# Graph attention on one core: values of two key blocks issued together ahead of the scores of every second step

## Chip, cores, metric

One core of one Trainium2 chip. The metric is device time in microseconds (us), median over runs. Runs of one kernel differ by up to some 0.2%. The traces show the array's clock halved for a few intervals of 3.4 us that fall differently in every run; over the runs of the kernel before, the mean granted clock lies between 0.996 and 0.999, and the shorter spans have the higher clock.

Engine names: PE is TensorE's matmuls, PEld its weight loads, DVE VectorE, ACT ScalarE, POOL GpSimd, SP SyncE (it issues most DMAs). L481 is line 481 of the kernel.

## The reference, cut

32 batches of 512 nodes with 512 features. Layer 0 is a graph convolution, layer 1 attention with 8 heads that sees only neighbours; each is added to its input and normalised.

```python
x = layernorm(x + deg * (x @ Wi.T + b) + adj @ (x @ Wj.T))
q, k, v = heads(x @ Wq.T + bq), heads(x @ Wk.T + bk), heads(x @ Wv.T + bv)   # 8 heads of 64
s = where(adj == 0, -inf, q @ k.T / 8)
x = layernorm(x + merge(softmax(s) @ v) @ Wo.T + bo)
```

## The kernel before

The attention of batch b runs in 8 steps, one for each half g of the heads (4 heads) and each block kc of 128 keys. Between the attention matmuls of a step the kernel places "pieces": products of the projections of neighbouring batches, spread over the steps so that PE always has work. Two PSUM buffers (mma, mmb) take the pieces in turn.

```python
    def scores(b, hp, kc):                        # two heads
        ps = sc_tile()                            # PSUM, two buffers
        for s in range(2):
            r = slice(s * HD, (s + 1) * HD)       # 64 rows of the array each
            nc.tensor.matmul(ps[:, s, :], KT[b, hp // 2][r, ...], QT[b, hp // 2][r, ...], ...)
        e = E[hp % 2, kc] = work([P, 2, N], "e", 4)
        nc.scalar.activation(ps, ps, AF.Exp, scale=QSCALE)              # L485
        nc.vector.tensor_tensor(e, ps, edge[...], op=OP.mult)           # L486: mask

    def values(b, g, kc):                         # four heads, 32 columns of the array each
        if kc == 0:
            PV[g] = [ov_tile(), ov_tile()]        # PSUM, two buffers in all
        for r in range(2):
            for h in range(4):
                nc.tensor.matmul(PV[g][r][32 * h:32 * h + 32, :], V[b][:, kc, c0:c0 + 32], E[h // 2, kc][...], ...)

    for n in range(1, B + 1):                     # cut: flushes, the last batch's exceptions
        b = n - 1
        for step in range(STEPS):
            g, kc = divmod(step, NC)
            scores(b, 2 * g, kc)
            scores(b, 2 * g + 1, kc)
            # pb, pg, pk: the step before
            values(pb, pg, pk)
            if pk == NC - 1:
                sums(pg)                          # L513: sums of exponentials, into a buffer of sc
                drain(pb, pg)                     # L518: ACT takes them out
                extra = rest(pb, pg)              # 4 reciprocals, 2 scalings into oT (L538), a check
            for f in PERIODS[n][step]: ...        # pieces, and small jobs of the other engines
```

## Time and profile before

| | before |
|---|---|
| median of 4 runs | 3709.5 us (3708.7 to 3709.9) |
| PE busy; share of the chain that ended last | 99%; 96% |
| DVE, POOL, ACT busy | 65%, 53%, 28% |
| values blocks between scores and pieces | 255 |

A line of the timeline gives start, length, engine, line, operation, output<-input, shape, count and, in brackets, the engine's idle time before it with what ended it. A float32 matmul leaves two records, so 8 matmuls of values show as x16. The lengths overlap from one record to the next: PE's pace is read from starts. The prediction below shows the page and the timelines.

### The profile page before, as it was taken

Reading aid. Unit: us, or ns where it says so; the run is one execution under the profiler, and the core shown is the slowest. Engines: PE = TensorE matmul, PEld = TensorE weight load, DVE = VectorE, ACT = ScalarE, POOL = GpSimd, SP = SyncE. Lnnn points to the kernel's source line nnn. Section 1 sums busy time; section 2 is a strip of 40 time slices with the busy share of each in tenths; the row PEclk is TensorE's granted clock in tenths of the full one; section 3 lists DMA queues with packets and bytes.
Section 4 is the critical chain, followed back from the end, with each engine's and each line's share of the span. In section 5 each row is a group of like instructions: output and inputs, shape, how many; then the busy total and the mean of one; then the engine's idle time right before and its main releaser. Section 6 shows DMA issues by size and latency. Waiting matters only on the chain.

```text
span 3706.9 us, 49623 instructions
## 1 busy us (share of the span) xinstructions
PE 3665.2 (99%) x18458; PEld 2511.4 (68%) x18458; DVE 2396.9 (65%) x3139; ACT 1029.1 (28%) x1482; POOL 1946.5 (53%) x1986
## 2 busy tenths in 40 slices
PE   8999999999999999999999999999999999999997
PEld 5666666666676767676666767676767666666763
DVE  4566766666666666666666666666666666666666
ACT  2222232222322222323233222222232332222322
POOL 3465545555455564455554555644555545556443
PEclk9999999999999999999999999999999999999999
DMA  7444556455555545554555544455545555445541
GB/s 250 125 126 133 151 151 162 124 141 138 152 159 145 128 135 150 153 160 120 141 142 154 159 141 130 134 151 157 157 122 139 141 159 157 137 132 137 151 131 44
DMA packets 797174, 530.02 MB, mean 143 GB/s; under 512 B 530433, under 2 KB 611841, under 8 KB 796929
## 3 DMA queue, kind: packets, MB, share of 16 engines
q1 hardware_dynamic: 780384, 494.78, 49.4%
q10 hardware_dynamic: 16320, 31.46, 2.3%
q8 instruction: 151, 2.47, 0.3%
q14 instruction: 95, 0.77, 0.1%
q0 software_dynamic: 224, 0.53, 0.0%
HBM read 453.25 MB, written 73.40 MB: 142 GB/s over the span
## 4 chain that ended last, share of the span: by engine, by line
PE 96%; DVE 1%; SPq 1%; POOL 1%; DMA 0%; issue 0%; ACT 0%; POOLq 0%; DVEq 0%; ACTq 0%
PE mma L427 31%; PE mmb L427 31%; PE sc L481 13%; PE ov L503 13%; PE mmb L325 3%; PE mma L325 3%; PE sc L513 2%; SPq L113 0%; DMA wv<-e 0%; DVE e L486 0%; DVE rl L522 0%; DVE st L289 0%; SPq L144 0%; PE sc L721 0%; SPq L166 0%
## 5 line engine op out<-in xcount | busy, mean ns | idle before, releaser
L485 ACT ACTIVATE sc<-sc 128x1024 f32<-128x1024 f32 x512 | 493.1, 1006 | 1538.4 <-PE sc L481 1532.2
L486 DVE TENSOR_TENSOR e<-sc,edge 128x1024 f32<-128x1024 f32 x512 | 602.5, 1218 | 211.4 <-ACT sc L485 180.4
L427 PE MATMUL mmb<-ring,big 128*128 128x256 f32 x3144 | 733.7, 382 | 3.1 <-issue 3.1
L427 PE MATMUL mma<-ring,big 128*128 128x256 f32 x3112 | 724.5, 381 | 3.9 <-ACT p L434 2.8
L427 PEld LDWEIGHTS mmb<-ring,big 128*128 128x128 f32 x3144 | 593.7, 190 | 134.1 <-issue 30.2
L427 PEld LDWEIGHTS mma<-ring,big 128*128 128x128 f32 x3112 | 585.7, 190 | 135.6 <-issue 27.0
L481 PE MATMUL sc<-q,k 64*128 64x512 f32 x2048 | 509.7, 616 | 0.0
L396 POOL TENSOR_TENSOR big<-big 128x512 f32<-128x512 f32 x376 | 493.1, 1339 | 29.3 <-ACT big L354 10.1
L503 PE MATMUL ov<-e,v 128*32 128x512 f32 x4096 | 494.0, 600 | 3.6 <-DVE oT L538 3.6
L492 POOL TENSOR_TENSOR es<-e 128x1024 f32<-128x1024 f32 x128 | 301.0, 2364 | 346.0 <-DVE e L486 346.0
L427 PE MATMUL mma<-big,ring 128*128 128x256 f32 x1808 | 431.5, 382 | 3.2 <-DVE k L465 3.2
L427 PE MATMUL mmb<-big,ring 128*128 128x256 f32 x1776 | 422.7, 381 | 0.0
L291 POOL TENSOR_SCALAR mv<-mv 128x1 f32<-128x1 f32 x256 | 51.0, 199 | 672.5 <-DVE mv L290 660.0
L427 PEld LDWEIGHTS mma<-big,ring 128*128 128x128 f32 x1808 | 341.0, 190 | 76.8 <-issue 25.1
L427 PEld LDWEIGHTS mmb<-big,ring 128*128 128x128 f32 x1776 | 334.5, 190 | 72.0 <-issue 25.1
L503 PEld LDWEIGHTS ov<-e,v 128*32 128x32 f32 x4096 | 107.1, 109 | 351.6 <-issue 321.7
L204 POOL TENSOR_TENSOR xlo<-xh,xhi 128x512 fp32r<-128x512 f32 x128 | 164.0, 1294 | 337.3 <-ACT xhi L203 337.2
L481 PEld LDWEIGHTS sc<-q,k 64*128 64x128 f32 x2048 | 176.5, 186 | 208.4 <-issue 205.4
L340 POOL TENSOR_TENSOR big<-big,deg_r 128x512 f32<-128x512 f32 x124 | 174.0, 1404 | 266.5 <-DVE big L339 266.5
L494 DVE TENSOR_TENSOR es<-es,e 128x1024 f32<-128x1024 f32 x251 | 307.7, 1227 | 0.0
L445 DVE TENSOR_TENSOR xh<-xh,mma 128x512 f32<-128x512 f32 x186 | 126.7, 681 | 269.7 <-PE mma L427 269.7
L445 DVE TENSOR_TENSOR xh<-xh,mmb 128x512 f32<-128x512 f32 x186 | 126.7, 681 | 262.6 <-PE mmb L427 262.6
(147 smaller groups left out, 3659.5 us busy)
## 6 DMA issues: line engine op xcount, KB each, us to landing
ring<-wo SPq DMA_DIRECT2D x217, 256.0 KB, 2.8
ring<-wq SPq DMA_DIRECT2D x160, 256.0 KB, 3.9
ring<-wv SPq DMA_DIRECT2D x160, 256.0 KB, 3.3
ring<-wk SPq DMA_DIRECT2D x160, 256.0 KB, 3.4
ring<-wi SPq DMA_DIRECT2D x155, 256.0 KB, 2.7
ring<-wj SPq DMA_DIRECT2D x155, 256.0 KB, 2.6
xh<-in_x_dram SPq DMA_DIRECT2D x32, 1024.0 KB, 5.5
xa<-in_x_dram SPq DMA_DIRECT2D x124, 256.0 KB, 3.9
```

What stands on the lines that cost most here:

```text
L204: nc.gpsimd.tensor_sub(lo, xs, hi.bitcast(FT))
L325: nc.tensor.matmul(pm, parts[w][:, jc, :], adjR[:, jc, :], start=(w == 0 and jc == 0), stop=(w == 1 and jc == NC - 1))
L340: nc.gpsimd.tensor_tensor(XD[b][:, dc, :], XD[b][:, dc, :], deg_r, op=OP.mult)
L396: nc.gpsimd.tensor_tensor(dst, p, q, op=OP.subtract)
L427: nc.tensor.matmul(pm[:, c * Q:(c + 1) * Q], lhs, rhs, start=first, stop=(kc == 1 and n == len(terms) - 1), skip_group_check=True)
L445: nc.vector.tensor_tensor(d, d, pm, op=OP.add)
L481: nc.tensor.matmul(ps[:, s, :], KT[b, hp // 2][r, hp % 2, kc * P:(kc + 1) * P], QT[b, hp // 2][r, hp % 2, :], start=True, stop=True)
L485: nc.scalar.activation(ps, ps, AF.Exp, scale=QSCALE)
L486: nc.vector.tensor_tensor(e, ps, edge[:, kc:kc + 1, :].to_broadcast([P, 2, N]), op=OP.mult)
L492: nc.gpsimd.tensor_add(ES[i], E[i, 0], E[i, 1])
L494: (eng or nc.vector).tensor_add(ES[i], ES[i], E[i, kc])
L503: nc.tensor.matmul(PV[g][r][32 * h:32 * h + 32, :], V[b][:, kc, c0:c0 + 32], E[h // 2, kc][:, h % 2, :], start=(kc == 0), stop=(kc == NC - 1))
```

## The change

The intent: every change between the array's cuts (64\*128 for scores, 128\*32 for values, 128\*128 for pieces) costs PE time. If the values of two steps stand together, every second step is spared one visit to the values' cut. Even steps issue the two waiting blocks, then their scores; odd steps issue scores alone. The last batch keeps the old order.

```diff
+    due = []
     for n in range(1, B + 1):
         ...
-            scores(b, 2 * g, kc)
-            scores(b, 2 * g + 1, kc)
-            pb, pg, pk = (b, *divmod(step - 1, NC)) if step > 0 else (b - 1, 1, NC - 1)
-            if pb >= 0:
-                values(pb, pg, pk)
-                ... sums, drain, rest after the last block
+            alone = b == B - 1 and step > 0
+            if alone:
+                scores(b, 2 * g, kc)
+                scores(b, 2 * g + 1, kc)
+            if alone or kc % 2 == 0:
+                for pb, pg, pk in due:
+                    values(pb, pg, pk)
+                    ... sums, drain, rest after the last block
+                due = []
+            due.append((b, g, kc))
+            if not alone:
+                scores(b, 2 * g, kc)
+                scores(b, 2 * g + 1, kc)
```

More of the change, by code (lines that the diff above doesn't have):

```diff
@@ L758, in gnn_attention_kernel @@
             g, kc = divmod(step, NC)
-            scores(b, 2 * g, kc)
-            scores(b, 2 * g + 1, kc)
-            pb, pg, pk = (b, *divmod(step - 1, NC)) if step > 0 else (b - 1, 1, NC - 1)
-            if pb >= 0:
-                values(pb, pg, pk)
-                if pk == NC - 1:
-                    sums(pg)
-                    drain(pb, pg)
-                    extra = rest(pb, pg)
+            alone = b == B - 1 and step > 0
[5 more added lines that the diff above has]
+                    values(pb, pg, pk)
+                    if pk == NC - 1:
+                        sums(pg)
+                        drain(pb, pg)
+                        extra = rest(pb, pg)
+                due = []
[3 more added lines that the diff above has]
+                scores(b, 2 * g + 1, kc)
             late = [(presum, i, kc) for i in range(2) if kc > 0]
```

## The prediction

> **What bounds the kernel now.** I read the page first: engine shares, then the chain that ended last.
>
> ```profile
> PE 3665.2 (99%) x18458; PEld 2511.4 (68%) x18458; DVE 2396.9 (65%) x3139; ACT 1029.1 (28%) x1482; POOL 1946.5 (53%) x1986
> PE 96%; DVE 1%; SPq 1%; POOL 1%; DMA 0%; issue 0%; ACT 0%; POOLq 0%; DVEq 0%; ACTq 0%
> ```
>
> PE is the bound from end to end: 99% busy and 96% of the chain. Only the time between PE's starts counts; other engines matter when they hold PE up. Next I looked at one step (there are 256, eight to each of 32 batches) in the timeline of PE alone. A step has a scores block (L481), a values block (L503), then "pieces", the products of the projections (L427, L325).
>
> ```profile
> 1823.14 1.99 PE L481 MATMUL sc<-q,k 64*128 64x512 f32 x8
> 1825.06 1.92 PE L503 MATMUL ov<-e,v 128*32 128x512 f32 x16
> 1826.91 0.48 PE L427 MATMUL mma<-ring,big 128*128 128x256 f32 x1
> ```
>
> The shapes 64\*128, 128\*32 and 128\*128 are three ways of cutting up the array. The timeline of weight loads gives the rhythm inside a block:
>
> ```profile
> 1823.68 0.19 PEld L481 LDWEIGHTS sc<-q,k 64*128 64x128 f32 x2 [0.24 <-issue]
> 1824.11 0.19 PEld L481 LDWEIGHTS sc<-q,k 64*128 64x128 f32 x2 [0.23 <-issue]
> 1825.06 0.16 PEld L503 LDWEIGHTS ov<-e,v 128*32 128x32 f32 x8 [0.76 <-issue]
> 1825.51 0.13 PEld L503 LDWEIGHTS ov<-e,v 128*32 128x32 f32 x4 [0.30 <-issue]
> ```
>
> Each block is four rounds 0.43 us apart, but its first round is longer: 0.54 us for scores (1823.14 to 1823.68), 0.45 us for values (1825.06 to 1825.51). And each block is longer than its rounds: scores 1.92 us from start to next block's start, values 1.85 us, against 4 x 0.43 = 1.72. A step whose values are followed by the sums of exponentials (L513, the same cut) shows what is absent when the cut stays:
>
> ```profile
> 1809.82 1.92 PE L503 MATMUL ov<-e,v 128*32 128x512 f32 x16
> 1811.56 1.04 PE L513 MATMUL sc<-es,ones 128*32 128x512 f32 x8
> ```
>
> Here values take 1.74 us, not 1.85: 0.11 us is the price of leaving the cut, and the remaining 0.02 to 0.03 is the longer first round. So a change of cut costs a drain (0.09 to 0.11 us) plus a first weight load that nothing hides (0.10 us for 128 columns, 0.026 us for 32). Over all steps I measured from PE's starts, piece to scores 0.197, scores to values 0.121, values to piece 0.217: nearly the same in all 250 cases. PE has almost no other lost time after the first 140 us.
>
> **What the Trainium skill says.** "TensorEngine Tiling (Array Packing)", Key Properties: changing the tiling mode drains the TensorE, using another tile of the same mode does not. The trace agrees: 1.85 against 1.74 us above. "TensorE: Matmul & The Clock Gate", LDWEIGHTS: a load costs its columns over 1.2 per ns, which is 107 ns for 128 columns and 27 for 32. The lengthened first rounds (about 0.105 and 0.026 us) agree, although a load's own record is longer (0.19). The same page, Part 1, has VectorE and ScalarE as strict FIFOs. The trace agrees: the vector engine's work below runs back to back in program order while PE needs the last item of it.
>
> **The change, part by part.** Today 255 values blocks stand each between scores and pieces. Afterwards the values of two steps stand together before the scores of every even step; odd steps have none. The last batch keeps the old order from its second step on. No matmul goes; 31 x 4 = 124 separate values blocks go, merged into a neighbour. A merged block pays no entry load and no exit drain: 0.026 + 0.11 = 0.138 us. The same sum by transitions (piece to values estimated at 0.091 + 0.026 = 0.117, values to scores at 0.217, scores to piece 0.200 as the very first step shows) is 136.6 us of switches before, 119.4 after. **Gain: 124 x 0.138 = 17.1 us.**
>
> Against it stands what moves. In odd steps nothing now lies between scores and pieces, so the pieces start 1.85 us sooner after the scores (1.92 us instead of 3.77). In even steps too the pieces follow the scores directly. The exponentials (ACT, L485) and the masking (DVE, L486) depend on the scores, so in both they end about 2.7 to 2.9 us after pieces begin, not 0.8 to 1.1. I therefore took every wait of PE on another engine and asked whether its slack beats 1.85 us; a bank's next load starts about 0.054 us after its reader ends, and a held first load adds its 0.105. In even steps I found enough room. Three places in odd steps do not:
>
> Step 7, timeline of DVE:
>
> ```profile
> 1797.39 2.35 DVE L486 TENSOR_TENSOR e<-sc,edge 128x1024 f32<-128x1024 f32 x2
> 1799.66 0.70 DVE L339 STREAM_TRANSPOSE big<-xa 128x512 f32<-128x512 f32 x1
> 1800.29 2.40 DVE L345 SCALAR_TENSOR_TENSOR xh<-b_r,deg_c,xh 128x512 f32<-128x512 f32 x2
> 1802.61 1.21 DVE L494 TENSOR_TENSOR es<-es,e 128x1024 f32<-128x1024 f32 x1
> 1803.74 0.68 DVE L465 TENSOR_TENSOR k<-mmb,k 128x512 f32<-128x512 f32 x1
> ```
>
> The queue has no gap, so bank mmb comes free at 1804.42, counted from scores that start at 1795.17. PE's next use of it is at 1806.08 today: 1.66 us of slack. Less 1.85 that is -0.19; with 0.054 and 0.105, PE stalls 0.35 us. Some 30 batches: 10.4 us.
>
> Step 3: the first piece (today at 1855.57) reads the turned activations that the transpose of L373 finishes at 1853.86 (1852.61 + 1.25). It would like to start at 1853.72: a stall of 0.14 + 0.054 = 0.19 us, 30 times: 5.8 us (its first load is exposed in any case).
>
> Step 5: masking ends at 1884.44; the add L465 behind it (0.69) would free mmb near 1885.05, while PE wants it at 1885.07 instead of 1886.92. With the load, a stall of about 0.15 us, 30 times: 4.5 us.
>
> One new wait: in steps 0 and 4 sums now come before the scores and take one of the two sc buffers, so the second scores tile waits until ACT has drained the sums (L518, 0.60 us and 0.09 more for its accumulator). From the recorded offsets the drain ends 0.14 us before PE wants the buffer; the held load makes it about 0.02 us, 62 times: 1.5 us.
>
> Sum: -17.1 + 10.4 + 5.8 + 4.5 + 1.5 = **+5 us**, that is 3714 us if every stall comes as worked out.
>
> **Rivals.** (a) Switches only: the stalls don't show, because DVE's items can run faster when they fall at other moments beside GpSimd (the pair of L345 takes 2.40 us here and 3.42 a step earlier, both with POOL busy). Then 3709 - 17 = 3692 us. For it: the switch costs are very regular and their number is exact. Against it: the three chains are recorded item by item, and an early step shows PE idle for 0.78 us on just such a DVE add (138.2 us). (b) The lag is larger than I think: a further wait that I take as covered binds, for instance L470 in step 4, whose bank would come free within 0.1 us of PE's need, or the drain holds both scores tiles (62 x 0.4 = 25 us). Then 3720 to 3740 us. (c) Waits of values on the scaled outputs vanish (L538 released weight loads in about 35 cases). I count nothing: these are idle times of the load path, while PE's own starts show no delay there.
>
> **Range and chances.** The two main terms are of the same size, 17 us for and 22 us against; I know the first better (within 5 us), the second within about 10. Weighing (a) at a third brings the centre to 3709 us. The range runs from (a) to the weak form of (b): 3692 to 3721. 2% is 74 us, which no path reaches except by a wait that I have missed altogether.
>
> **What would show it.** Right: the PE timeline shows 32 values records in one block of about 3.57 us, scores going straight over to pieces in 1.92 us, fewer separate blocks (131); in odd steps idle of PE or its weight load put down to DVE L465 (steps 5 and 7) and L373 (step 3), with sums near 15, and 5 us. Wrong: values blocks no shorter per step than today (then the piece-to-values switch costs more than 0.12 us); no PE idle behind L465 and L373 (rival a); or large waits on ACT L518, L470 or POOL (rival b).

## More of the kernel before

Lines of the periods that matter later (z marks a job that is no piece):

```python
 # phase_a, steps 6 and 7: gathers (L325) g, pieces k, transposes, bias additions (base, L345)
            res += g[i:i + 1] + k[i:i + 1] + [z(l0_turn, n, i)]
            if i in (1, 2):
                res += [z(base, n, i - 1)]
 # phase_b, end of step 1 and step 2 (DVE comes to h_turn in step 3): layer 0 is normalised (apply, L296, ACT), stored to HBM (L360), read
 # back in another layout (L367) and transposed by DVE (h_turn, L373), for the projections
        ... *project(m, 7), z(apply, n, 0), z(h_store, n, 0), l0[5], z(h_load, n, 0), z(add_bo, n - 1, 1), *project(m, 4),
            l0[3], z(stats, n, 1), z(h_turn, n, 0), *project(m, 5)]
 # phase_c, from step 3: v[1] is the first piece that reads the transpose
```

## The result, and the profile after

| | before | after |
|---|---|---|
| median of 4 runs | 3709.5 us | 3755.2 us (3753.8 to 3758.1) |
| ratio to before | 1 | 1.0126 (95% interval 1.0111 to 1.0141) |

A ratio is the mean time of one kernel's fast runs over that of the other's fast runs of the same rounds, so not quite the ratio of these medians. The kernel became 46 us slower: within 2%, but clear of noise, and outside the predicted range.

Page after, engine shares and chain:

```profile
PE 3666.4 (98%) x18458; PEld 2515.1 (67%) x18458; DVE 2391.5 (64%) x3139; ACT 1030.6 (27%) x1482; POOL 1957.5 (52%) x1986
PE 79%; DVE 9%; issue 5%; POOL 4%; ACT 1%; SPq 1%; DMA 0%; POOLq 0%; DVEq 0%; ACTq 0%
```

PE has the same work, but the chain is now PE's for only 79% and runs through DVE, POOL and ACT for the rest: PE waits for others. The switches themselves did what was intended. Timeline of PE after, an even step:

```profile
1854.41 1.89 PE L427 MATMUL mmb<-ring,big 128*128 128x256 f32 x8
1856.23 3.64 PE L503 MATMUL ov<-e,v 128*32 128x512 f32 x32
1859.80 1.99 PE L481 MATMUL sc<-q,k 64*128 64x512 f32 x8
1861.72 1.56 PE L427 MATMUL mma<-ring,big 128*128 128x256 f32 x6
```

Two blocks of values take 3.57 us from start to next start, against 2 x 1.85 before, and the scores hand over to pieces in 1.92. Over all of PE's starts, piece to values costs 0.117 us (124 times), values to scores 0.217, scores to piece 0.200, as the estimate had it.

To find the loss I compared all starts of PE with the pace of the blocks and the cost of the switch between them, and booked the rest by step of the batch. Batches 2 to 31, in us of PE time:

| where PE waits beyond pace and switches | before | after |
|---|---|---|
| step 3, first piece (29 waits) | 0 | 33.9 |
| step 7, last piece | 0 | 15.0 |
| step 5, third piece | 0 | 5.2 |
| steps 0 and 4, second scores (drain of the sums) | 0 | 1.2 |

These 55.3 us, the saved switches of -17.2, and 3.4 us in the first batch, where two transposes of layer 0 wait for an sc buffer, make 41.5 of the 45.0 us by which the profiled spans differ (3706.9 and 3751.9). Of the rest, 1.6 us are a longer wait in the last batch; what is left is no more than a mean clock of 0.996 instead of 0.997 could make (some 4 us), which was not tested.

**Step 3.** Its chain begins in step 2. Timeline before, steps 2 and 3 of one batch:

```profile
1838.65 1.93 ACT L485 ACTIVATE sc<-sc 128x1024 f32<-128x1024 f32 x2 [12.40 <-PE sc L481]
1840.47 1.51 ACT L296 ACTIVATE xh<-xh,mv 128x512 f32<-128x512 f32 x2
1842.02 0.37 ACTq L360 DMA_DIRECT2D hd<-xh  x1
1844.13 0.32 SPq L277 DMA_DIRECT2D ring<-wo  x1
1844.99 0.99 SPq L277 DMA_DIRECT2D ring<-in_wvT_dram  x1
1846.09 3.43 SPq L367 DMA_DIRECT2D xa<-hd  x4
...
1852.61 1.25 DVE L373 STREAM_TRANSPOSE big<-xa 128x1024 f32<-128x1024 f32 x1
...
1855.57 1.99 PE L427 MATMUL mma<-ring,big 128*128 128x256 f32 x8
```

Timeline after, the same steps:

```profile
1860.98 1.93 ACT L485 ACTIVATE sc<-sc 128x1024 f32<-128x1024 f32 x2 [14.12 <-PE sc L481]
...
1862.80 1.51 ACT L296 ACTIVATE xh<-xh,mv 128x512 f32<-128x512 f32 x2
1864.35 0.37 ACTq L360 DMA_DIRECT2D hd<-xh  x1
1864.61 0.32 SPq L277 DMA_DIRECT2D ring<-wo  x1
1865.47 0.38 SPq L277 DMA_DIRECT2D ring<-in_wvT_dram  x1
...
1868.04 2.93 SPq L367 DMA_DIRECT2D xa<-hd  x4
...
1874.46 1.25 DVE L373 STREAM_TRANSPOSE big<-xa 128x1024 f32<-128x1024 f32 x1 [1.38 <-DMA xa<-hd]
1875.81 1.97 PE L427 MATMUL mma<-ring,big 128*128 128x256 f32 x8 [1.55 <-issue]
```

Read from the start of step 2's first piece (1841.24 before, 1861.72 after). The normalisations (L296) stand behind the two exponentials (L485) in ACT's queue, so the store leaves at 0.78 before and at 2.63 after: 1.85 us later, as the scores are. From here on the figures are medians over the batches, unless marked as those of the batch shown. The store also takes longer to land, 3.6 us against 2.8: two loads of weights (L277) are now issued 0.3 and 1.1 us behind it, where before one came 2.1 us behind. The reload starts at 6.3 instead of 4.2 (4.9 in the batch shown) and lands at 12.1 instead of 10.5. Before, DVE reached the transpose at 11.4, with the data there; now it waits for them (the bracket 1.38 <-DMA) and ends at 13.4 (in the batch shown 14.0), while the scores of step 3 have made room for the piece at 12.5. "1.55 <-issue" is the label of that wait: the profile found no releaser, but the transpose's end (1874.46 + 1.25 = 1875.71) is 0.1 us ahead of the piece.

**Step 7** is the queue shown in the prediction. Timeline after:

```profile
1815.40 1.99 PE L481 MATMUL sc<-q,k 64*128 64x512 f32 x8
...
1817.80 2.34 DVE L486 TENSOR_TENSOR e<-sc,edge 128x1024 f32<-128x1024 f32 x2
...
1824.12 0.68 DVE L465 TENSOR_TENSOR k<-mmb,k 128x512 f32<-128x512 f32 x1
...
1824.85 1.35 PE L427 MATMUL mmb<-big,ring 128*128 128x256 f32 x5 [0.23 <-DVE k L465]
```

The k addition frees mmb at 1824.80 and PE starts 0.05 us later; the bracket names the releaser. The table's figure for this wait is larger than the bracket's 0.23, because matmul records reach past the next start and the exposed first load comes on top: 0.40 + 0.10 us in the starts.

### The profile page after: what moved, and what is told of

Read it like the earlier page. It is cut to its first block, busy times and chain, and to the rows that moved or that the text cites. A ratio compares the mean times of both kernels' runs of the same rounds, so it can differ in the third digit from the quotient of the medians.

```text
span 3751.9 us, 49654 instructions
## 1 busy us (share of the span) xinstructions
PE 3666.4 (98%) x18458; PEld 2515.1 (67%) x18458; DVE 2391.5 (64%) x3139; ACT 1030.6 (27%) x1482; POOL 1957.5 (52%) x1986
## 4 chain that ended last, share of the span: by engine, by line
PE 79%; DVE 9%; issue 5%; POOL 4%; ACT 1%; SPq 1%; DMA 0%; POOLq 0%; DVEq 0%; ACTq 0%
PE mma L427 26%; PE mmb L427 26%; PE ov L503 12%; PE sc L481 11%; DVE xh L345 3%; POOL xlo L204 2%; DVE e L486 2%; PE sc L513 2%; POOL big L340 1%; DVE es L494 1%; DVE k L465 1%; PE mmb L325 1%; PE mma L325 1%; DVE big L339 1%; ACT big L331 0%
## 5 line engine op out<-in xcount | busy, mean ns | idle before, releaser
L485 ACT ACTIVATE sc<-sc 128x1024 f32<-128x1024 f32 x512 | 494.1, 1006 | 1515.0 <-PE sc L481 1514.4
L503 PE MATMUL ov<-e,v 128*32 128x512 f32 x4096 | 467.8, 596 | 4.1 <-DVE oT L538 4.1
L204 POOL TENSOR_TENSOR xlo<-xh,xhi 128x512 fp32r<-128x512 f32 x128 | 176.4, 1389 | 335.3 <-ACT xhi L203 335.3
L503 PEld LDWEIGHTS ov<-e,v 128*32 128x32 f32 x4096 | 119.8, 109 | 279.6 <-issue 272.2
L442 POOL TENSOR_TENSOR xh<-xh,p 128x512 f32<-128x512 f32 x186 | 231.3, 1277 | 0.0
L522 DVE RECIPROCAL rl<-rl 128x128 f32<-128x128 f32 x252 | 224.7, 924 | 1.6 <-ACT rl L518 1.6
```

The costliest lines, as they stand in the source:

```text
L204: nc.gpsimd.tensor_sub(lo, xs, hi.bitcast(FT))
L442: nc.gpsimd.tensor_tensor(d, d, p1, op=OP.add)
L522: nc.vector.reciprocal(RL[g][1][:, c], RL[g][src][:, c])
```

## The experiments

Eleven kernels, all correct. Each row compares with the kernel before, run in the same rounds on the same chip.

| run | median us | ratio, 95% interval |
|---|---|---|
| the change | 3755.2 | 1.0126 (1.0111 to 1.0141) |
| e1_apply_ahead | 3730.3 | 1.0064 (1.0047 to 1.0081) |
| e2_base_late | 3739.4 | 1.0089 (1.0072 to 1.0106) |
| e3_unmerged | 3779.0 | 1.0194 (1.0177 to 1.0211) |
| e4_steps123_old | 3723.5 | 1.0047 (1.0030 to 1.0064) |
| e5_all_mended | 3726.0 | 1.0050 (1.0036 to 1.0063) |
| e6_before_mended | 3714.2 | 1.0016 (1.0002 to 1.0029) |
| e7_merged_behind | 3717.0 | 1.0024 (1.0008 to 1.0039) |
| e8_best | 3695.6 | 0.9968 (0.9954 to 0.9981) |
| e9_behind_mended | 3701.2 | 0.9981 (0.9968 to 0.9995) |
| e10_before_mended2 | 3707.2 | 1.0001 (0.9988 to 1.0015) |
| e11_ahead_mended | 3701.7 | 0.9985 (0.9972 to 0.9999) |

### e1: the normalisations of step 2 ahead of its scores

```diff
             due.append((b, g, kc))
+            todo = PERIODS[n][step]
+            while step == 2 and not alone and n > 1 and todo and ... todo[0][1] in (apply, h_store):
+                run(todo.pop(0))
             if not alone:
                 scores(b, 2 * g, kc)
```

> The changed kernel, with the two normalisations (L296) and the store of the activations in step 2 issued ahead of that step's scores, not behind them; nothing else. My theory: 36 of the 46 us lost are one wait in step 3, where the first piece stands 1.1 to 1.2 us in 29 batches because the normalisations queue on ACT behind the two exponentials, which come 1.85 us later relative to the pieces than before, so that store, reload and transpose all end late. Then this run takes back 33 to 36 us: 3719 to 3723 us, and the wait at the first piece of step 3 falls from 1.17 us to about 0.2 (the DVE queue alone). Rival, the reload is late because the DMA queues are fuller or slower in the changed kernel (its store lands in 3.6 us, before in 2.8): then an earlier issue helps little, 3745 us or more.

Measured: 0.6% slower than before where the change was 1.3%, so about half taken back. Timeline of e1, steps 2 and 3:

```profile
1848.69 0.81 ACT L296 ACTIVATE xh<-xh,mv 128x512 f32<-128x512 f32 x1 [10.70 <-POOL mv L293]
1849.96 0.81 ACT L296 ACTIVATE xh<-xh,mv 128x512 f32<-128x512 f32 x1 [0.46 <-POOL mv L293]
1850.81 0.37 ACTq L360 DMA_DIRECT2D hd<-xh  x1
...
1864.21 1.25 DVE L373 STREAM_TRANSPOSE big<-xa 128x1024 f32<-128x1024 f32 x1
...
1865.56 0.67 PE L427 MATMUL mma<-ring,big 128*128 128x256 f32 x2 [0.17 <-PE sc L481]
```

The normalisations now fill ACT's idle time while PE does values; the store lands in 2.8 us again, the transpose no longer waits for data in most batches, and the wait at the first piece falls from 33.9 to 7.9 us in sum (0.27 us each, expected 0.2). So the wait begins with the ACT order, and what is left is the DVE queue of the prediction. The rival is not refuted altogether: the store leaves 4.7 us earlier than in the change and is thereby clear of the weight loads too, so this run can't tell the later leaving from the slower landing (see what stays open, below). I had expected 33 to 36 us back and got 23 to 25: I had booked 36 us on step 3, where PE's starts show 33.9, of which 26.0 went.

### e2: bias additions out of the queue of step 7

```diff
-            if i in (1, 2):
-                res += [z(base, n, i - 1)]
+            if i in (1, 3):
+                res += [z(base, n, i // 2)]
```

> The changed kernel, with the second pair of bias additions (L345) moved behind the step's k addition and transpose, out of the DVE queue between masking and k addition in step 7. My theory: PE's 0.5 us wait in step 7 (30 batches, 15 us in the trace) is that queue, so the wait goes and the time falls to 3739 to 3742 us. Rival: it is only one of several waits that shadow each other, and the time stays at 3755, or the later additions hold up POOL and PE in the next step.

Measured 3739.4, as the theory had it: the waits of step 7 fall from 15.0 us to 0.2, and nothing shadowed them. Two other differences of this trace nearly cancel: step 3 waits 27.4 us, not 33.9 (its reload lands at 11.8 instead of 12.1), and the last batch waits some 7 us more.

### e3: the order without the merging

```diff
-            if alone or kc % 2 == 0:
+            if True:
```

> Values ahead of the scores in every step, one block each as before the change: the order of the change without its merging, so no switch of cut is saved (P to O, O to S, S to P is 0.534 us, before 0.535). My theory: the waits of steps 7 and 5 (15 and 5 us) and the sums' drain (1 us) stay, since pieces follow 1.92 us after the scores; the wait of step 3 goes, since its pieces are not earlier relative to the store of step 2 (the transpose ends 13.5 us after the pieces of step 2 began, the first piece of step 3 is due at 14.3). So 3709 + 21 + up to 4 of the first batch = 3728 to 3736 us. Rival, the loss comes from merging alone (odd steps without values): about 3710 us. Rival, it comes from the order alone: 3755 us and more.

Missed: 72 us slower than before, not 19 to 27. The wait at the first piece of step 3 is gone as expected (1.7 us left), step 7 has 10 us where 15 were expected, step 5 has none where 5 were, and later pieces of step 3 have 9 us that were not expected. Above all, a wait appears that neither theory named; from the waits of e3:

```profile
PE ov L503 <- DVE oT L538: 47.6, 33, 2.8
```

(engine and line, releaser: us in total, times, longest). The first values of g = 1 take the ov buffers that the scaling L538 empties. Put ahead of the scores of step 5 they come before it ends, 1.48 us in each of 30 batches, 44 us. Without it e3 would stand at 3735, inside the expectation, though partly because the other misses cancel. In the change itself merging moves these values to step 6, so the wait can't arise. The two halves of the change thus need each other, and this run alone can't say what merging costs; e7 does.

### e4: the old order in steps 1 to 3

```diff
-            alone = b == B - 1 and step > 0
+            alone = b == B - 1 and step > 0 or step in (1, 2, 3)
```

> The changed kernel with steps 1, 2 and 3 of every batch in the old order (values of one block behind the scores), so that only the blocks of steps 4 and 5 and of steps 6 and 7 are merged. My theory: the 41 us of step 3 go, the waits of step 7 and 5 stay (20 us), half of the switches saved stay (62 x 0.138 = 8.6 us): 3709 + 20 + 1 - 9 = 3721 us, between 3717 and 3726. Rival, the loss is spread over all merged steps: half of 46, 3732 us.

Measured 3723.5, within the expected band, 9 us from the rival's figure. Step 3 has no wait at its first piece, step 7 keeps 15.2 us and step 5 5.2. The loss sits in these places and isn't spread over all merged steps.

### e7: merged, but behind the scores

```diff
-            if alone:
+            if True:
                 scores(b, 2 * g, kc)
                 scores(b, 2 * g + 1, kc)
 ...
-            if not alone:
-                scores(b, 2 * g, kc)
-                scores(b, 2 * g + 1, kc)
```

> The changed kernel with the two blocks of values behind the scores of the even step, not ahead of them; the odd steps have none, as in the change. Tells merging from order. Theory: the exponentials of step 2 then come no later than before against the normalisations, so the store leaves early and the wait in step 3 shrinks from 1.17 us to about 0.2; steps 7 and 5 keep their waits (15 and 5 us), switches save 17: 3709 - 17 + 6 + 15 + 5 + 1 = 3719 us, between 3712 and 3726. Rival, odd steps without values are the cost whatever the order: 3750 us.

Measured 3717.0. The store of step 2 leaves 0.95 us before the step's pieces begin, not 2.63 after, and the first piece of step 3 waits 8.4 us in sum; steps 7 and 5 keep 10.2 and 4.5. So with merged blocks, putting them behind the scores instead of ahead takes back some 38 of the 46 us. Neither half of the change alone makes the wait of step 3 what it is: e3, with the order and no merging, has 1.7 us at that piece, e7, with merging and no such order, 8.4, and both together 33.9.

### e5 and e6: everything mended, and a control

e5 is the change with the edits of e1 and e2 and these:

```diff
-                l0[3], z(stats, n, 1), z(h_turn, n, 0), *project(m, 5)]
+                l0[3], z(h_turn, n, 0), z(stats, n, 1), *project(m, 5)]
-            alone = b == B - 1 and step > 0
+            alone = b == 0 or b == B - 1 and step > 0
+            late, held = late + held, []          # ahead of the step's pieces
+            if step == 4 and 0 < b < B - 1:       # after them: two scalings and the check wait
+                held, extra = extra, []
```

> The changed kernel with every wait that it brought taken out: normalisations and store of step 2 ahead of its scores (as in the run that tried this alone), the second bias additions behind the k addition (likewise), the transpose of step 3 ahead of the statistics, the output scaling left over in step 4 held until behind the masking of step 5, and the first batch in the old order. My theory: PE's waits in steps 3, 5 and 7 fall to about the level of the kernel before, 120 merged blocks save 120 x 0.138 = 16.6 us, the sums' drain costs 1 us: 14 to 17 us faster than before, ratio 0.9955 to 0.9963. Rival, the merging itself has a cost that I don't see in the waits: ratio 1.000 or above.

> Control: the kernel before with the same side edits (normalisations and store of step 2 ahead of the scores, bias additions later, transpose ahead of the statistics, the last check of step 4 held until step 5) but values of one block behind every step's scores, as before. PE had no waits there, so nothing can be won: within 3 us of before, ratio 0.999 to 1.001. If it were 10 us faster, the gain of the mended version would not be the merging's.

e5 missed: 18 us slower than before. Steps 5 and 7 are clean (0.3 and 0.2 us), so holding the scaling works, but step 3 has 37 us of waits, 34 of them new ones in its later pieces. From the waits of e5:

```profile
PEld mma L427 <- ACT p L434: 20.8, 16, 1.7
PEld mmb L427 <- ACT p L434: 15.9, 14, 1.5
```

With the transpose first, DVE stands waiting for the reload (2.16 us in the batch I looked at), the statistics come late, hence the normalisations of step 3 on ACT, and behind them in ACT's queue the copy L434 that a piece needs. One wait had become another. The control e6, which has the same edit, missed its range too: it is 0.16% slower than before. The sums of step 4 wait in 10 batches, 9.3 us; which of its edits makes them wait was not isolated.

### e8 to e11: the versions without that edit, and their control

e8 is e7 with later bias additions, the held scaling, the first batch in the old order, and for step 3:

```diff
-    z(apply, n, 0), z(h_store, n, 0), l0[5], z(h_load, n, 0), ...
-    l0[3], z(stats, n, 1), z(h_turn, n, 0), *project(m, 5)]
+    z(apply, n, 0), z(h_store, n, 0), z(h_load, n, 0), l0[5], ...
+    l0[3], z(stats_of, n, 2), z(h_turn, n, 0), z(stats_of, n, 3), *project(m, 5)]
```

e9 is e8 without this last edit; e11 is the change's own order with the edits of e1 and e2, the held scaling and the first batch in the old order, which is e5 with the transpose back in its place and nothing else; e10 is the kernel before with e8's side edits (of the held jobs only the check) and no merging.

> Two blocks of values behind the scores of the even steps (as in the run that tried this), the second bias additions behind the k addition, the output scaling of step 4 held until step 5, the first batch in the old order, and for step 3 the reload issued one piece earlier and the transpose between the two statistics. Expected: waits of steps 3, 5 and 7 at the level of before, so that the 120 merged blocks' 16.6 us stay: 13 to 17 us faster, ratio 0.9955 to 0.9965. If the reload issued earlier blocks the loads behind it, waits in step 2 or 3 take it back: ratio 0.998 to 1.002.

> The same without the two edits for step 3 (reload and transpose where they were): steps 5 and 7 free of waits, the first piece of step 3 still waits about 0.28 us for the transpose in 29 batches: 16.6 - 8.4 = 8 us faster, ratio 0.997 to 0.9985.

> The change's own order, values of two blocks ahead of the scores, with normalisations and store of step 2 ahead of these scores, later bias additions, held scaling and the first batch in the old order, but the transpose left behind the statistics (moving it there had cost 40 us in waits of ACT in step 3). Waits left: 8 us in step 3, 1 us at the sums: 16.6 - 9 = 7 us faster, ratio 0.997 to 0.999.

> Control: the kernel before with the side edits of the best version (bias additions later, one check held, transpose between the statistics, reload one piece earlier) and nothing merged. PE had no waits in these places: within 3 us of before, ratio 0.999 to 1.001.

e9, e10 and e11 came out inside their expected ratios. e11 has 12 us of waits in step 3 against e5's 37, so the transpose ahead of the statistics was what cost e5 its gain. e8 fell just short of its range (12 us and 0.9968, expected 13 to 17 and 0.9955 to 0.9965, which its interval covers); it is the fastest kernel. Its page:

```profile
PE 3654.9 (99%) x18458; PEld 2520.3 (68%) x18458; DVE 2405.5 (65%) x3139; ACT 1028.7 (28%) x1482; POOL 1982.4 (54%) x1986
PE 96%; DVE 1%; SPq 1%; POOL 1%; DMA 0%; issue 0%; ACT 0%; POOLq 0%; DVEq 0%; ACTq 0%
```

The chain is PE's again. The control e10 doesn't differ from before, so the gain of e8 is not that of the side edits which e10 has; what e8 has besides is the merging, with the held scaling and the first batch's order that go with it. The gain is 12 us (0.33%), not the whole 16.6: e8's trace has 6.4 us more waits than the control's in the later pieces of step 3.

## Why the prediction was wrong, point by point

**What bounds the kernel, and the price of a switch:** right. Every transition cost what was estimated (0.117, 0.217 and 0.200 us), 124 blocks were merged, the term of -17 us stands; e8, with 120 blocks merged, shows most of it as time against e10.

**Step 7, 10.4 us:** right in mechanism, mis-sized: 15.0. The bracket of a line before that shown (L345 <-POOL xlo, 0.42 us, before the change 0.21) makes the DVE queue start 0.18 us later than I carried over: masking starts 2.40 us after the scores' start, before 2.22. Where it still starts at 2.22, in e3 and e7, the wait is 10 us, as predicted. e2 removed the wait by emptying this queue.

**Step 5, 4.5 us, and the drain of the sums, 1.5 us:** right, 5.2 and 1.2.

**Step 3, 5.8 us:** this is the step that failed. I named the right producer (the transpose L373) and the right consumer, but carried over its end from the trace of before, where DVE's queue set it. The prediction says: "In even steps I found enough room." There was none in step 2: I asked only which waits of PE on an engine had slack, one link deep. The normalisations there stand behind the exponentials in ACT's queue, and their slack lay three links away from PE, at store, reload and transpose. With the store leaving 1.85 us later and taking 0.8 us longer, the reload became the transpose's bound, and instead of 0.19 us PE waits 1.17. e1 (ACT order alone), e4 (old order in these steps) and e7 (scores first) each remove 25 to 34 us of it. It was not among the forms named in rival (b), though its direction was. Rival (a), that stalls would not show, is refuted: all three did.

**Missed besides:** 3.4 us in the first batch, where transposes of layer 0 follow scores directly. The first-batch order of e8 avoids it.

**What stays open:** how much of step 3's wait is the later leaving of the store and how much its slower landing. In the three kernels where it leaves at 2.63 (the change, e2, e3), two weight loads follow it by 0.3 and 1.1 us and it lands in 3.6; in all the others no load follows it so soon and it lands in 2.8. That points to these loads, but no run moved them alone. Had the store landed in 2.8, the reload would by an estimate from the medians above have landed near 11.2, just before DVE comes to the transpose at 11.4, and most of the 1.17 us would not have arisen. So the 1.85 us alone would nearly have fitted; what they made the store meet did not. The share of the granted clock is only compared, not tested.

## What to carry to other kernels

In this kernel, where one engine is busy to 99%, moving its work gained 17 us in itself and cost 55 through results that now leave earlier or later on the other queues. For each moved result follow everything behind it in the in-order queues to the next use on the bound engine, through DMAs too, and compare the lag with the slack of the whole chain and not of its last link; look also at which transfers a moved transfer will meet. Grouping work of one array cut paid here (0.33%) once small jobs of the other engines were moved along with it.

## What the Trainium skill lacked or had wrong

- "TensorEngine Tiling (Array Packing)", Key Properties, says that a change of mode drains the array but gives no figure. Here it costs 0.09 to 0.11 us, and the first weight load on top: 0.117 us from a 128\*128 to a 128\*32 cut, 0.121 from 64\*128 to 128\*32, 0.197 to 0.217 into 64\*128 or 128\*128.
- "TensorE: Matmul & The Clock Gate", LDWEIGHTS: columns over 1.2 (107 and 27 ns) agrees with the exposed time of a first load (105 and 26 ns), but not with the load's record in the profile, which shows 186 and 110 ns. That section does not say which of the two its formula means.
- The same page says that ACT and DVE queues are strict FIFOs. No page that I used adds the consequence that cost most here: a store behind an exponential in ACT's queue delays its reload and all that waits for it (1.85 us at the store, with a landing slower by 0.8 us, became 1.17 us of PE's time in 29 batches).
